# Storing three of four input groups by line, and reading them by unit

## The chip, the core and the metric

The kernel runs on one NeuronCore of a Trainium2 chip. The metric is device time in microseconds of that core; the kernel before takes 4201.34 us (median of three runs, 4199.3 to 4201.84).

## The reference

The input x is (32, 48, 64, 128), that is batch, channel, row h, column w, float32. Two layers follow each other. Each is `x = x + scnn(groupnorm(x))`, with its own weights:

```python
nxt = inp + conv1d(carry, w, b)      # 48 to 48 channels, 5 taps
```

The SCNN part runs this step along h from 0 to 63 (carry is a whole row, the taps run over w), then back from 63 to 0, then along w from 0 to 127 (carry is a column, the taps run over h), then back. Every step needs the one before it. The group norm has 16 groups of three channels and takes mean and variance over its channels and all of h and w, per image.

## The kernel before

**Tiling.** The 32 images are four groups of eight (`GB`). Channel and position modulo eight give 48 x 8 = 384 rows, three tiles `o` of 128 partitions; `PIECES` (L50) says which channels of which residue `e` lie where: ten pieces of 16, 32 or 48 partitions. A step (L876) is nine products of 128x128 on TensorE and three additions on VectorE (L898), one for each `o`.

**Phases.** `PHASES` (L103) are 12: eight "rows" phases (one image group each, 63 steps down and 63 up) and four "cols" phases (a pair of groups, 127 steps right and 127 left). This text counts them from 0. Their order is rows of layer 0 for groups 0 and 1, cols for that pair (phase 2), rows of group 2 (phase 3), rows of layer 1 for group 0 (phase 4), rows of layer 0 for group 3 (phase 5), cols for groups 2 and 3 (phase 6), rows of layer 1 for groups 1, 2, 3 (phases 7 to 9), and the two cols of layer 1. The tile names in the profile tell them apart: `step_02d` is layer 0, group 2, down.

**The input of layer 0.** An image group of x comes in as it lies in memory, 24 rows on each partition (`take_in`, tensor `in_x`). GpSimd copies two of these rows at a time into the order (quarter, residue, block, image) (`permute`, L650 to L659), and `put_out` (L661) stores each of the 24 permuted rows to a DRAM tensor `xin` of that group in one DMA of 128 partitions, 512 KB, issued on SyncE's queue SP. For group 0 this is done at the start, by GpSimd and ScalarE; for groups 1, 2 and 3 `plan_input` (L981) puts it beside the scans, through two tiles of two rows each. ScalarE takes the group's statistics from the same input tiles (`take_others`, L512).

**Reading it.** xin is laid out by (residue or row block, quarter), channel, and then a unit of 8 KB. It is read twice. A rows phase of layer 0 loads its 64 rows in four blocks of 16: `move_rows` (L679) issues 20 DMAs a block in runs of 128 bytes, ten for every eight rows. ScalarE then normalizes the block (`scale_rows`, L714, 24 ACTIVATE on L722, images outermost and `o` innermost), and the scan reads one row per step. A cols phase of layer 0 loads x again as a residual (`load_residual`, L810): for each quarter and each of six units (three `o`, two groups) it issues three or four DMAs, one for each piece, with 8 KB contiguous on each partition. GpSimd adds it (L824), `keep_result` (L826) stores the sum to `mid`, the input of layer 1, and statistics of the sum are taken. `mid` is laid out by quarter, line, (position, channel) and line content. Layer 1 reads it with `take_rows` (L702), which issues 40 DMAs for a block of 16 rows, one for each piece and quarter, in runs of 128 bytes, and with `by_unit` (L246), which covers a 1 MB unit of 128 partitions in one DMA, or two for the last `o`, in runs of 1 KB.

**What sets the order.** `at` (L968) enters work in an agenda under a time counted in steps; `catch_up` hands it out as the steps are traced, and `in_order` (L277) ties every instruction to the one before on its engine. Each queue therefore issues in program order. The agenda's time isn't waited for: a queue runs ahead until an instruction of it waits for data or for a buffer. Nearly all DMAs are on SP. The tile layer gives DMAs of SP and ScalarE eight completion semaphores in turn, and a DMA waits until the last one with its semaphore has landed, so that at most eight are in flight. `plan_rows` (L1001) places block loads and scalings of a rows phase: phase 1 loads at -34, -18, -3 and +12 steps of its start, a rows phase after a cols phase at -28, -12, 4 and 20, others at -54, -43, 0 and 11. It also places the stores of the finished up-scan (`upa`, ten DMAs for eight rows).

Of the kernel before, what the change touches and what calls it, by code (L numbers as in the profile page):

```python
# [29 lines left out]
F32 = mybir.dt.float32  # L30
# [3 lines left out]
C = 48  # L34
# [8 lines left out]
E8 = 8  # L43
FULL = 128
NG = E8 * C // FULL
NQ = 4
# [31 lines left out]
def weight_runs():  # L78
# [24 lines left out]
PHASES = (  # L103
    ("rows", 0, 0),
    ("rows", 0, 1),
    ("cols", 0, 0),
    ("rows", 0, 2),
    ("rows", 1, 0),
    ("rows", 0, 3),
    ("cols", 0, 1),  # L110
    ("rows", 1, 1),
# [8 lines left out]
def kernel(  # L120
# [8 lines left out]
    nc = tc.nc  # L129
    B, _, H, W = x.shape  # L130
    NK = W // E8
    NH = H // E8
# [4 lines left out]
    LINE = E8 * RUN  # L137
    UNIT = NH * LINE
    SLOT = 2 * NG * UNIT
    HALF = H // 2  # L140
    NGRP = B // GB
# [4 lines left out]
    PR = C * H // FULL  # L146
# [6 lines left out]
    dram = ctx.enter_context(tc.tile_pool(name="dram", bufs=1, space=bass.MemoryType.DRAM))  # L153
# [34 lines left out]
    def kept(name):  # L188
# [3 lines left out]
            for g in range(NGRP)  # L192
        ]

    source = [
        [
            dram.tile([E8 * NQ, C, UNIT], F32, tag=f"xin{g}", name=f"xin{g}")
            for g in range(NGRP)
        ],
        [  # L200
            dram.tile([NQ, NH, E8 * C, LINE], F32, tag=f"mid{g}", name=f"mid{g}")
            for g in range(NGRP)
        ],
    ]
    ups = [kept("upa"), kept("upb")]
    taps = [
# [28 lines left out]
    def x_by_col(t, e, j):  # L235


        return t[e * NQ + j]
# [7 lines left out]
    def by_unit(t, o, j):  # L246


        at = [(o * FULL, 0, FULL)]
        if o == NG - 1:  # L250
            at = [(6 * C, 0, 2 * C), (5 * C + C // 3, 2 * C, FULL)]
        t = t[j].rearrange("a m n -> m a n")
        return [(t[r : r + p1 - p0], p0, p1) for r, p0, p1 in at]

    def by_line(t):

        return t.rearrange("p (a n) -> p a n", a=NH)

    def x_put(t, r):


        t = t.rearrange("(i q) c (a n) -> i (c a) q n", i=E8, a=NH)[r % E8]
        return t.rearrange("(p r) q n -> r p q n", r=PR // E8)[r // E8]
# [6 lines left out]
    def dma(dst, src, queue=None):  # L270
        (queue or nc.sync).dma_start(dst, src)
# [34 lines left out]
    def pieces(o):  # L306
        return [(e, c0, c1, p0) for e, c0, c1, g, p0 in PIECES if g == o]
# [342 lines left out]
    def permute(nat, r0, perm, engines):  # L650
# [4 lines left out]
        for i in range(rows * NQ):  # L655
# [2 lines left out]
            copy = eng.copy if eng is nc.scalar else eng.tensor_copy  # L658
            copy(dst[:, r, q], src[:, r0 + r, q])  # L659

    def put_out(g, r, perm):  # L661


        n = perm.shape[-1] // (W * GB)
        for i in range(n):
            at = slice(i * W * GB, (i + 1) * W * GB)
            dma(
                x_put(source[0][g], r + i),
                perm[:, at].rearrange("p (q n) -> p q n", q=NQ),
            )  # L670


    def row_views(k):
# [2 lines left out]
    def row(k, h):  # L676
        return row_views(k)[h // HALF][:, :, h % HALF]
# [132 lines left out]
    def load_residual(k, j, i, nat):  # L810
        _, layer, pair = PHASES[k]
        o, half = UNITS[i]
        t = source[layer][2 * pair + half]
        if layer:
            for there, p0, p1 in by_unit(t, o, j):
                dma(by_line(nat)[p0:p1], there, nc.scalar)
        else:
            for e, c0, c1, p0 in pieces(o):
                dma(nat[p0 : p0 + c1 - c0], x_by_col(t, e, j)[c0:c1])
# [148 lines left out]
    def at(t, fn, *args):  # L968
        agenda.append((t, len(agenda), fn, args))
# [11 lines left out]
    def plan_input(g, times, work, lag, nats, perms):  # L981

        stats = InputStats(f"x{g}", 0)
        rows = nats[0].shape[-1] // W
        ahead, pieces_of = len(nats), rows * W // BN
        per = rows * W * GB // perms[0].shape[-1]
        for j, t in enumerate(times):
            nat = nats[j % ahead]
            if j == 0 and g > 1:
                at(t - 7, take_in, g, 0, nat)  # L990
            for i in range(per):
                perm, r = perms[i % len(perms)], i * rows // per
                at(t + i * work / per, permute, nat, r, perm, [nc.gpsimd])
                at(t + i * work / per + 4, put_out, g, rows * j + r, perm)
            at(t + lag, stats.take_others, pieces_of * j, nat)
            if j + ahead < len(times):
                free = t + 7
                at(free, take_in, g, rows * (j + ahead), nat)
        spread(t + work + lag + (0, 2, 32, 5)[g], scaling(f"x{g}", 0, g, stats, x_masks, (0, 0, 8, 0)[g]), 1)

    def plan_rows(k, t0, prev):  # L1001
        if k == 1:
            ahead, scaled = (-34, -18, -3, 12), (-12, -2, 17, 33)
        elif prev == "cols":
            ahead, scaled = (-28, -12, 4, 20), (-13, 3, 19, 35)
        else:
            ahead, scaled = (-54, -43, 0, 11), (-22, -8, 16, 30)
        if k:
            for i in range(4):
                if PHASES[k][1]:  # L1010
                    for o in range(NG):
                        t = t0 + ahead[i] - 2 + 3 * o
                        at(t, take_rows, k, i * LOAD, (i + 1) * LOAD, o)
                else:
                    at(t0 + ahead[i], move_rows, k, i * LOAD, (i + 1) * LOAD, False)
                at(t0 + scaled[i], scale_rows, k, i * LOAD, (i + 1) * LOAD)

        cuts = list(range(0, H + 1, E8))
        following = PHASES[k + 1][0] == "cols"
        seam = following and follows(k + 1)  # L1020
        if seam:
            cuts = cuts[2:]
            end = t0 + 2 * (H - 1)
            at(end - E8, move_rows, k, E8, 2 * E8, True, 0)
            for h in range(E8 - 1, -1, -1):
                at(end - h, send_row, k + 1, h, range(0, E8 // 2))
            at(end, send_rest, k + 1, range(E8 // 2, E8))
            for q in range(1, NQ):
                at(end + 0.1 if q == 1 else end + 1.6, move_rows, k, 0, 2 * E8, True, q)
        for h0, h1 in zip(cuts, cuts[1:]):  # L1030
            t = t0 + 2 * (H - 1) - h0
            if k == 0:
                t += 16 if h0 >= HALF else 68
            elif not following:
                t = t0 + 92 + 5 * (H - h1) / E8 + (34 if h1 <= HALF else 0)
            at(t, move_rows, k, h0, h1, True)
        at(
            t0 + H - 1,
            nc.gpsimd.tensor_copy,
            last.rearrange("p (o n) -> p o n", o=NG),  # L1040
            row(k, H - 1),
        )

    def follows(k):

        _, layer, pair = PHASES[k]
        return PHASES[k - 1] == ("rows", layer, 2 * pair + 1)

    def plan_cols(k, t0, prev):
# [44 lines left out]
        for u, (t, j, i) in enumerate(direct):  # L1094
            nat = tiles[u % n]
            o, half = UNITS[i]
            if u < n:
                at(left + 16, load_residual, k, j, i, nat)
            if layer == 0:
                if u >= n:  # L1100
                    at(direct[u - n][0] + 3, load_residual, k, j, i, nat)
                at(t, add_residual, k, j, i, nat)
                at(t + 4, keep_result, k, j, i)
                unit = quarter(k, j)[:, half, o]
                if half == 0:
                    for b in range(GB):
                        at(t + 5 + b, stats[0].take, j, o, unit, b)
                else:
                    at(t + 1, stats[1].take, j, o, unit)
            else:  # L1110

                at(t, add_residual, k, j, i, nat)
                at(t + 2.5, permute_unit, k, j, i, nat, (nc.gpsimd, nc.scalar, nc.scalar))
                if final or j not in HELD:
                    at(t + 4.5, store_result, k, j, i, nat)
                else:
                    at(t + 4.5, hold_result, j, i, nat)
                if final and j == 1:
                    at(t + 4.7, load_residual, k, 0, i, last_tiles(k)[i])

                if u >= 2 and u - 2 + n < len(direct):
                    at(t + 4.6, load_residual, k, *direct[u - 2 + n][1:], tiles[(u - 2) % n])
# [60 lines left out]
    def first_group():  # L1183
# [84 lines left out]
        def put_rows(*engines):  # L1268
            for eng in engines:
                r, perm = order[put[0]], tiles[put[0]]  # L1270
                put[0] += 1
                permute(parts[r // rows], r % rows, perm, (eng,))
                put_out(0, r, perm)
# [142 lines left out]
```

## Time and profile before

| | |
|---|---|
| profiled execution, device time | 4201.03 us |
| its span, first to last instruction | 4199.2 us |
| mean granted TensorE clock | 0.987 |
| GpSimd, ScalarE, VectorE busy | 19%, 31%, 51% |
| SP queue (q1): packets, data, share of 16 DMA engines | 2062096, 582.09 MB, 68.2% |
| ScalarE queue (q10) | 141424, 87.19 MB, 8.6% |
| stores to xin, 512 KB each | 96 |
| phase 1, 3, 4, 5, 7: TensorE's first step | 332.3, 1090.1, 1361.1, 1613.2, 2368.4 us |

Busy shares are of the span. In a timeline, a line is a run of like instructions: start, duration, engine, line of code, tensors, count; `SPq` is the SP queue, whose time is that of issuing, waits for semaphores included. A helper issues nearly all DMAs, so that they all carry one line of code (L271), and the tensors tell them apart. A window's row has the busy time of each engine, the granted clock, the busy share of the DMA engines and the data moved.

### The profile page before, as it was taken

The page shows a single profiled execution, that of the slowest core. Times are in us where ns is not written, and L with a number is a line of the kernel's source. Part 1 is how long each engine was busy: PE and PEld are TensorE (multiplying, and loading weights), DVE is VectorE, ACT ScalarE, POOL GpSimd, SP SyncE. Part 2 cuts the span into 40 slices and gives each one's busy share as a digit, 9 for nine tenths or more (in the row PEclk, how much of TensorE's full clock was granted, in tenths as well). Part 3 has the DMA queues.
Part 4 walks back from the last instruction along what each step waited for, and adds up shares of the span by engine and source line. Part 5 has one row for each costly group of instructions (what it writes and reads, how often), then busy time and mean ns, then how long its engine had stood idle before and what let it go on. Part 6 is the DMA issues. An engine that isn't in the chain of part 4 may idle for free. (4 is left out here: it accounts for less than half of the span.)

```text
span 4199.2 us, 90284 instructions
## 1 busy us (share of the span) xinstructions
PE 4083.1 (97%) x36724; PEld 4050.4 (96%) x36724; DVE 2133.5 (51%) x6501; ACT 1287.7 (31%) x2525; POOL 787.0 (19%) x737
## 2 busy tenths in 40 slices
PE   8999999999999999999999999999999999999994
PEld 6999999999989999999999989999999999999994
DVE  5454444456644454444457554444444444444444
ACT  6845000536874543000016762523000002200122
POOL 3520010434222000010023410000000006610253
PEclk9999999999999999999999999999999999999997
DMA  9987669669969999258419968948379019999799
GB/s 293 235 178 115 110 125 209 210 162 250 206 186 165 168 166 157 36 104 195 99 44 264 187 142 140 139 65 141 64 130 212 14 51 232 287 253 160 152 237 197
DMA packets 2206497, 680.57 MB, mean 162 GB/s; under 512 B 2008465, under 2 KB 2157185, under 8 KB 2179969
## 3 DMA queue, kind: packets, MB, share of 16 engines
q1 hardware_dynamic: 2062096, 582.09, 68.2%
q10 hardware_dynamic: 141424, 87.19, 8.6%
q8 instruction: 289, 4.73, 0.5%
q0 software_dynamic: 2560, 5.51, 0.5%
q14 instruction: 128, 1.04, 0.1%
HBM read 397.77 MB, written 295.14 MB: 165 GB/s over the span
## 5 line engine op out<-in xcount | busy, mean ns | idle before, releaser
L722 ACT ACTIVATE arena<-arena,offset,scale 128x256 f32<-128x256 f32 (+2 forms) x840 | 582.5, 789 | 377.2 <-DMA arena<-mid 230.7
L824 POOL TENSOR_TENSOR arena<-arena 128x2048 f32<-128x2048 f32 x80 | 362.8, 4548 | 1456.3 <-PE step_10l L889 463.1
L659 POOL COPY arena<-arena 128x256 f32<-128x256 f32 x332 | 196.7, 657 | 460.3 <-DMA arena<-in_x 407.5
L597 ACT ACTIVATE early<-arena 128x256 f32<-128x256 f32 x192 | 129.5, 675 | 442.0 <-POOL arena L824 436.1
L889 PE MATMUL step_00r<-arena,early 128*128 128x128 f32 x2286 | 252.1, 274 | 6.1 <-DMA arena<-arena 5.8
L889 PEld LDWEIGHTS step_00r<-arena,early 128*128 128x128 f32 x2286 | 251.4, 185 | 6.8 <-issue 5.6
L889 PE MATMUL step_01r<-arena,early 128*128 128x128 f32 x2286 | 251.9, 274 | 6.2 <-DMA arena<-arena 5.2
L889 PEld LDWEIGHTS step_01r<-arena,early 128*128 128x128 f32 x2286 | 251.1, 185 | 7.0 <-issue 5.5
L889 PE MATMUL step_00l<-arena,wleft 128*128 128x128 f32 x2286 | 249.2, 272 | 0.0
L889 PE MATMUL step_11r<-arena,early 128*128 128x128 f32 x2286 | 249.2, 272 | 0.0
L889 PEld LDWEIGHTS step_11r<-arena,early 128*128 128x128 f32 x2286 | 248.7, 184 | 0.4 <-DVE arena L898 0.3
L889 PEld LDWEIGHTS step_00l<-arena,wleft 128*128 128x128 f32 x2286 | 248.7, 184 | 0.0
L889 PE MATMUL step_11l<-arena,wleft 128*128 128x128 f32 x2286 | 248.5, 272 | 0.0
L889 PE MATMUL step_10l<-arena,wleft 128*128 128x128 f32 x2286 | 248.5, 272 | 0.0
L889 PE MATMUL step_01l<-arena,wleft 128*128 128x128 f32 x2286 | 248.4, 272 | 0.0
L889 PE MATMUL step_10r<-arena,early 128*128 128x128 f32 x2286 | 248.4, 272 | 0.0
L889 PEld LDWEIGHTS step_11l<-arena,wleft 128*128 128x128 f32 x2286 | 248.4, 184 | 0.0
L889 PEld LDWEIGHTS step_10l<-arena,wleft 128*128 128x128 f32 x2286 | 248.4, 184 | 0.0
L889 PEld LDWEIGHTS step_01l<-arena,wleft 128*128 128x128 f32 x2286 | 248.4, 184 | 0.0
L889 PEld LDWEIGHTS step_10r<-arena,early 128*128 128x128 f32 x2286 | 248.4, 184 | 0.0
L282 ACT COPY early<-arena 128x1 f32<-128x1 f32 x2 | 0.4, 192 | 697.3 <-DVE arena L898 697.3
L846 ACT COPY arena<-arena 128x256 f32<-128x256 f32 x172 | 99.8, 657 | 362.5 <-POOL arena L824 277.2
(200 smaller groups left out, 7089.5 us busy)
## 6 DMA issues: line engine op xcount, KB each, us to landing
xin<-arena SPq DMA_DIRECT2D x91, 512.0 KB, 4.2
arena<-in_x SPq DMA_DIRECT2D x18, 2048.0 KB, 11.3
arena<-xin SPq DMA_DIRECT2D x96, 384.0 KB, 10.2
arena<-mid SPq DMA_DIRECT2D x384, 96.0 KB, 3.1
upb<-arena SPq DMA_DIRECT2D x192, 192.0 KB, 3.9
arena<-upb SPq DMA_DIRECT2D x96, 384.0 KB, 13.2
arena<-xin SPq DMA_DIRECT2D x180, 192.0 KB, 4.4
mid<-arena SPq DMA_DIRECT2D x32, 1024.0 KB, 10.6
```

Source lines behind the costliest of these rows:

```text
L282: fn(*args)
L597: nc.scalar.activation(junk[:, 0:n], view[:, b], AF.Identity, accum_out=self.sum[:, i, j : j + 1])
L659: copy(dst[:, r, q], src[:, r0 + r, q])
L722: nc.scalar.activation(args[0], args[0], AF.Identity, bias=args[2], scale=args[1])
L824: eng.tensor_tensor(unit, unit, nat, ALU.add)
L846: copy(by_w(perm)[:, a], src[:, a])
L889: nc.tensor.matmul(part(whole(ps[o])[0:m], -s), weights[:, i, at : at + m], part(src(i), s), start=seen[o] == 1, stop=seen[o] == left[o],)
```

## The change

The tensors xin of groups 1, 2 and 3 take the layout that mid has. Group 0 keeps its own.

```diff
+    def by_lines(name):
+
+        return dram.tile([NQ, NH, E8 * C, LINE], F32, tag=name, name=name)
+
     source = [
         [
-            dram.tile([E8 * NQ, C, UNIT], F32, tag=f"xin{g}", name=f"xin{g}")
+            by_lines(f"xin{g}")
+            if g
+            else dram.tile([E8 * NQ, C, UNIT], F32, tag=f"xin{g}", name=f"xin{g}")
             for g in range(NGRP)
         ],
...
+    def put_lines(t, r, perm):
+
+
+        i, runs = r % E8, PR // E8
+        t = t.rearrange("q a (i c) n -> i a c q n", i=E8)[i]
+        for first in range(E8):
+            c, a = divmod(runs * first + r // E8, E8)
+            dma(t[a, c : C : runs], perm[first : FULL : E8])
+
     def put_out(g, r, perm):
...
-            dma(
-                x_put(source[0][g], r + i),
-                perm[:, at].rearrange("p (q n) -> p q n", q=NQ),
-            )
+            whole = perm[:, at].rearrange("p (q n) -> p q n", q=NQ)
+            if g:
+                put_lines(source[0][g], r + i, whole)
+            else:
+                dma(x_put(source[0][g], r + i), whole)
...
         t = source[layer][2 * pair + half]
-        if layer:
+        if layer or pair or half:
             for there, p0, p1 in by_unit(t, o, j):
-                dma(by_line(nat)[p0:p1], there, nc.scalar)
+                dma(by_line(nat)[p0:p1], there, nc.scalar if layer else None)
...
-                if PHASES[k][1]:
+                if PHASES[k][1:] != (0, 0):
                     for o in range(NG):
                         t = t0 + ahead[i] - 2 + 3 * o
                         at(t, take_rows, k, i * LOAD, (i + 1) * LOAD, o)
```

So for groups 1 to 3 a permuted row goes out in eight DMAs of 16 partitions and 64 KB, still in runs of 1 KB; a residual unit comes in by one or two DMAs in runs of 1 KB, still on SP; and the row blocks of phases 1, 3 and 5 are loaded by `take_rows`, 40 DMAs a block in three portions, one for each `o`, which stand at -2, +1 and +4 steps of where the whole block stood.

More of the change, by code (lines that the diff above doesn't have):

```diff
@@ L193, in kept @@
         ]
+    def by_lines(name):
+        return dram.tile([NQ, NH, E8 * C, LINE], F32, tag=name, name=name)
     source = [
         [
-            dram.tile([E8 * NQ, C, UNIT], F32, tag=f"xin{g}", name=f"xin{g}")
+            by_lines(f"xin{g}")
+            if g
+            else dram.tile([E8 * NQ, C, UNIT], F32, tag=f"xin{g}", name=f"xin{g}")
             for g in range(NGRP)
         ],
[L200 to L203, printed above, removed]
+        [by_lines(f"mid{g}") for g in range(NGRP)],
     ]
```

## The prediction, before the changed kernel was run

> **What bounds the kernel now.** First the page's busy times and slices:
>
> ```profile
> PE 4083.1 (97%) x36724; PEld 4050.4 (96%) x36724; DVE 2133.5 (51%) x6501; ACT 1287.7 (31%) x2525; POOL 787.0 (19%) x737
> ...
> PE   8999999999999999999999999999999999999994
> ...
> DMA  9987669669969999258419968948379019999799
> ```
>
> TensorE sets the time, and nothing in the change touches its work. The change can only remove or make stalls of the scans. Those show in the phases' lengths, from the tiles of the down-scans (first start, last start of 63 steps):
>
> ```profile
> L889 PEld LDWEIGHTS step_01d<-arena,early x1134: 163/192/193, 332.1 to 456.5; 128*128 128x128 f32 x126, 128*96 128x96 f32 x63
> L889 PEld LDWEIGHTS step_02d<-arena,early x1134: 162/192/338, 1090.0 to 1230.5; 128*128 128x128 f32 x126, 128*96 128x96 f32 x63
> L889 PEld LDWEIGHTS step_11d<-arena,early x1134: 163/192/338, 2368.3 to 2519.8; 128*128 128x128 f32 x126, 128*96 128x96 f32 x63
> L889 PEld LDWEIGHTS step_12d<-arena,early x1134: 163/192/193, 2649.7 to 2775.1; 128*128 128x128 f32 x126, 128*96 128x96 f32 x63
> ```
>
> A clean scan takes some 125 us (1.98 a step). Phase 3 takes 140.5 and phase 7 151.5: 15.5 and 26.5 us are stalls. Both follow a cols phase whose residual loads share SP with the row blocks. In phase 7 ScalarE's scaling of rows 16 to 31 shows what is late:
>
> ```profile
> 2375.85 0.86 ACT L722 ACTIVATE arena<-arena,offset,scale 128x256 f32<-128x256 f32 x1
> 2378.69 0.85 ACT L722 ACTIVATE arena<-arena,offset,scale 128x256 f32<-128x256 f32 x1 [1.98 <-DMA arena<-mid]
> 2393.22 16.39 ACT L722 ACTIVATE arena<-arena,offset,scale 128x256 f32<-128x256 f32 x22 [13.68 <-DMA arena<-mid]
> ```
>
> The third instruction needs the last o, so a block is ready 16.5 us after its last portion lands, here at 2409.6; row 16 was due at 2368.4 + 15 x 1.98 = 2398. Next, SP before phase 1, where group 1 is stored:
>
> ```profile
> 181.22 7.42 SPq L271 DMA_DIRECT2D xin<-arena  x4
> ...
> 202.02 33.41 SPq L271 DMA_DIRECT2D xin<-arena  x14
> 235.52 10.85 SPq L271 DMA_DIRECT2D upa<-arena  x10
> 246.47 1.35 SPq L271 DMA_DIRECT2D xin<-arena  x2
> 251.74 20.28 SPq L271 DMA_DIRECT2D arena<-xin  x20
> 272.11 21.12 SPq L271 DMA_DIRECT2D upa<-arena  x20
> ```
>
> From 181 to 450 SP hardly rests. Phase 1 doesn't stall: its blocks are scaled at 298.5 and 334.7, due at 332.3 and 362.
>
> **What the skill says.** "DMA: Bandwidth & Descriptors", section "Rules for kernel authors": small transfers should be joined; under 64 KB one pays mostly overhead. The trace agrees: DMAs of 6 KB from SP stand 0.46 us apart at the closest, 1 MB ones 0.47. "SBUF — State Buffer", section "Door 1: The DMA port swizzle", says that bandwidth depends on how many of 16 ports the partitions reach, and partitions 0 to 63 reach half of them. Piece loads of 16 to 48 partitions (first row) against units of 128 (second) agree:
>
> ```profile
> 866.00:880.00 14.00, 14.00 (x131) 14.00 (x131) 7.02 (x23) 0.00 (x0) 0.00 (x0) 1.00 1.02 179
> 3412.00:3422.00 10.00, 10.00 (x95) 10.00 (x93) 4.80 (x15) 0.00 (x0) 0.00 (x0) 1.00 1.04 331
> ```
>
> Both have the DMA engines full; the last number is GB/s. "TensorE: Matmul & The Clock Gate", Part 1: an idle TensorE falls to half clock and needs some 3.4 us of work to recover. Phase 3's first two steps after its stall take 3.95 and 3.0 us instead of 1.97, so I add 3 us to each new stall.
>
> **The stores.** Of 72 stores each becomes eight: 504 more DMAs on SP. Bytes and runs stay, so the DMA engines don't feel it; SP does. A DMA of 64 descriptors isn't in the trace. Bounds: 0.41 us (shortest issue of a 512 KB store, 0.36, and the gap of 0.05) and 0.57 (a row DMA of mid). I take the floor of small DMAs, 0.47: 3.76 us a row. GpSimd needs less:
>
> ```profile
> 178.74 18.98 POOL L659 COPY arena<-arena 128x256 f32<-128x256 f32 x32
> ```
>
> That is eight rows, 2.37 each. So SP, not GpSimd, paces the stores. Group by group:
>
> *Group 1.* 24 x 3.76 = 90.2 us from 181.2; two loads of in_x in between, 1 us, and 4 us each until the semaphores behind a 2 MB load come free (9.4 to land, less the 3.3 in which seven stores go out; bounds 0 and 6); ten upa stores, 10.9; landing 2.2. The first row load starts at 293.5 instead of 251.7. A block by take_rows is 24.5 us:
>
> ```profile
> 1234.47 13.06 SPq L271 DMA_DIRECT2D early<-taps  x25
> ...
> 1285.78 3.46 SPq L271 DMA_DIRECT2D xin<-arena  x4
> ...
> 1364.09 49.04 SPq L271 DMA_DIRECT2D arena<-mid  x80
> ```
>
> 80 DMAs, two blocks; 40 DMAs of the old form take some 43, so reading costs 3 us more a block. But by the agenda the portions stand at steps 90, 93, 96, and upa stores at 94, 102 and 110: ten now fall ahead of the last portion. Block 0: 293.5 + 17.2 (28 DMAs) + 10.9 + 7.4 = 329.0, landed 332, scaled 348.5: 16 us late. Block 1 has the stores of 102 ahead and those of 110 inside: 329.0 + 10.9 + 17.2 + 10.9 + 7.4 = 375.4, scaled 394.9, due at 348.5 + 29.7 = 378.2: 17 more. Blocks 2 and 3 make it (419 against 426). Phase 1 loses 33 + 2 x 3 = 39 (bounds 20 and 55).
>
> *Group 2.* SP waits there for in_x and ScalarE; each four rows take 15 us instead of 7.4 and delay the next load by some 4.5, the last row by 27, to 886. The residuals that follow are added from 902 on, and the first lands within 6 us. Nothing; without this cover it would be under 10.
>
> *Group 3.* Rows 0 to 3 fall in an idle stretch. Rows 4 to 7 and 8 to 11 go out as in the fence, 3.4 us for four; now 15 each: +23 for SP's row blocks of phase 4. Rows 32 to 47 are scaled at 1407.8, due at 1361.1 + 31 x 1.99 = 1423: 15 us of slack. Late by 8, + 3 = 11 (bounds 0 and 18). The last 12 rows put SP some 55 us back before phase 5, whose rows 32 to 47 had 54 us of slack plus the 8 of phase 4: nothing, at most 7.
>
> **The residuals.** At 179 GB/s a unit of 1 MB takes 5.8 us of all DMA engines, at 331 3.2. Phase 2 has 10 such units after the first four, phase 6 has 20: 26 and 52 us less, and four DMAs for ten in SP's way. What is late in the stalls: in phase 3 rows 32 to 47, landed at 1151.6 and due (16.5 before the row) at 1135; in phase 7 rows 16 to 31, 2393 against 2381.5, then rows 32 to 47, 2438 against 2413. The relief exceeds each lack. What is late next is ScalarE's order of scaling and statistics (18 and 13.7 us in turn): it makes row 32 of phase 7 at 2426 against 2430. The portions, however, put a residual load ahead of the last o. I take 12 of phase 3's 15.5 (bounds 0 and 15.5) and 23 of phase 7's 26.5 (bounds 8 and 26.5).
>
> **The sum.** +39 + 11 - 12 - 23 = +15 on the profiled execution's 4201.0 (span 4199.2, 1.8 around it), 0.3 below the median of the runs: 4216.
>
> **Rivals.** *The reads win.* If an eighth of a row costs SP 0.41 us and in_x holds nothing up, phase 1's block 0 is in time, block 1 13 us late, 16 with the clock; phase 4 loses 7; the full 41 or so come back: 4184. It decides at about 0.41 us a store: 15 us over 192 DMAs for phase 1 and 64 for phase 4. For it: eight small DMAs leave the engines free. Against: no DMA of the trace goes out closer than 0.46. *The reads give nothing,* because the stalls of phases 3 and 7 come from order (a portion behind a residual that waits for GpSimd): +50, 4251. For it: SP waits 253.6 us for the residual additions. Against: the waits of ScalarE there end with DMAs, with the engines full. *Even.* Both sides within 8 us of each other: 4203.
>
> **How the numbers follow.** About 0.2%, 8.4 us, is what a measurement of this kernel can tell from no change. Forecast of a net loss 0.42; reads give nothing 0.12; even 0.18; reads win 0.28. So slower 0.54, same 0.18, faster 0.28. Range: 4183 takes in the reads winning, 4254 nearly all of the case with nothing back; the loss alone would be 4210 to 4240.
>
> **What would show it.** Right: stores to xin 0.47 us apart; phase 1 some 164 us down instead of 124.4, with TensorE idle ahead of rows 1 and 16; phase 3 near 128, phase 7 near 129, phase 4 near 136; residual units at over 300 GB/s. Wrong: phase 1 without a stall, or phases 3 and 7 as before.

## The result, and the profile after

The changed kernel takes 4342.4 us (median of four runs, 4332.8 to 4349.9) where the kernel before takes 4201.6 beside it: 1.033 times, 95% interval 1.0305 to 1.0355. The forecast was 4216, with 4254 as its upper end. The profiled execution is 4349.94 us with a span of 4348.2 and a mean granted clock of 0.972, to be set against 4201.03, 4199.2 and 0.987: 148.9 us more. It is the slowest of the four; by the medians the difference is 140.8 us. Lines of the changed kernel's code stand 3 to 13 below those of before (L271 is now L274, L659 is L662, L722 is L735, L824 is L837, L889 is L902, L898 is L911).

The page after, busy times and slices:

```profile
PE 4102.7 (94%) x36724; PEld 4066.9 (94%) x36724; DVE 2137.8 (49%) x6501; ACT 1286.9 (30%) x2525; POOL 787.0 (18%) x737
...
PE   8994999998988988999999999999999999999994
...
DMA  9748677749985866946914896957649317999799
```

The work of the engines is the same; TensorE now has gaps in slices 4, 10, 12, 13, 15 and 16, and the DMA engines are busy for five to nine tenths of these, so TensorE does not wait there for full DMA engines. The scans' tiles of the changed kernel say which (first start, last start):

```profile
L902 PEld LDWEIGHTS step_01d<-arena,early x1134: 163/192/338, 379.6 to 521.4; 128*128 128x128 f32 x126, 128*96 128x96 f32 x63
L902 PEld LDWEIGHTS step_02u<-arena,early x1134: 163/192/337, 1329.4 to 1473.2; 128*128 128x128 f32 x126, 128*96 128x96 f32 x63
L902 PEld LDWEIGHTS step_10d<-arena,early x1134: 163/192/337, 1473.3 to 1622.5; 128*128 128x128 f32 x126, 128*96 128x96 f32 x63
L902 PEld LDWEIGHTS step_10u<-arena,early x1134: 163/192/338, 1622.6 to 1768.2; 128*128 128x128 f32 x126, 128*96 128x96 f32 x63
L902 PEld LDWEIGHTS step_11d<-arena,early x1134: 163/192/338, 2529.3 to 2668.6; 128*128 128x128 f32 x126, 128*96 128x96 f32 x63
```

Phase 1 starts 47.5 us later and takes 141.8; phase 3 up, phase 4 down and phase 4 up take 143.8, 149.2 and 145.6 where some 125 to 130 were enough; phase 7 down takes 139.3, better than 151.5 but not the 129 of the forecast. SP ahead of phase 1, in the changed kernel:

```profile
181.17 21.64 SPq L274 DMA_DIRECT2D xin<-arena  x32
...
203.71 24.67 SPq L274 DMA_DIRECT2D xin<-arena  x32
...
229.81 79.50 SPq L274 DMA_DIRECT2D xin<-arena  x112
309.41 9.89 SPq L274 DMA_DIRECT2D upa<-arena  x10
319.40 10.98 SPq L274 DMA_DIRECT2D xin<-arena  x16
330.62 15.79 SPq L274 DMA_DIRECT2D arena<-xin  x28
346.51 9.13 SPq L274 DMA_DIRECT2D upa<-arena  x10
355.68 7.13 SPq L274 DMA_DIRECT2D arena<-xin  x12
```

The order is the one that the prediction worked out (28 loads, ten upa stores, 12 loads), but the first row load goes out at 330.6 and not at 293.5. Over all 576 stores the median from one issue to the next is 0.64 us, not 0.47.

### The profile page after: what moved, and what is told of

The parts are those of the page before. It is cut to its first block, busy times and chain, and to the rows that moved or that the text cites. A ratio compares the mean times of both kernels' runs of the same rounds, so it can differ in the third digit from the quotient of the medians.

```text
span 4348.2 us, 91103 instructions
## 1 busy us (share of the span) xinstructions
PE 4102.7 (94%) x36724; PEld 4066.9 (94%) x36724; DVE 2137.8 (49%) x6501; ACT 1286.9 (30%) x2525; POOL 787.0 (18%) x737
## 5 line engine op out<-in xcount | busy, mean ns | idle before, releaser
L735 ACT ACTIVATE arena<-arena,offset,scale 128x256 f32<-128x256 f32 (+2 forms) x840 | 581.9, 788 | 532.3 <-DMA arena<-mid 239.8
L837 POOL TENSOR_TENSOR arena<-arena 128x2048 f32<-128x2048 f32 x80 | 362.5, 4546 | 1422.4 <-PE step_10l L902 473.3
L662 POOL COPY arena<-arena 128x256 f32<-128x256 f32 x332 | 196.8, 647 | 657.7 <-DMA arena<-in_x 485.8
L902 PE MATMUL step_00l<-arena,wleft 128*128 128x128 f32 x2286 | 251.2, 273 | 21.0 <-DVE arena L911 21.0
L902 PEld LDWEIGHTS step_00l<-arena,wleft 128*128 128x128 f32 x2286 | 250.4, 185 | 21.2 <-DVE arena L911 21.2
L902 PE MATMUL step_00r<-arena,early 128*128 128x128 f32 x2286 | 253.8, 275 | 9.3 <-DMA arena<-arena 5.7
L902 PEld LDWEIGHTS step_00r<-arena,early 128*128 128x128 f32 x2286 | 253.1, 186 | 10.0 <-issue 5.0
L902 PE MATMUL step_01r<-arena,early 128*128 128x128 f32 x2286 | 253.6, 275 | 9.3 <-DMA arena<-arena 5.5
L902 PEld LDWEIGHTS step_01r<-arena,early 128*128 128x128 f32 x2286 | 252.9, 186 | 10.0 <-issue 5.5
L902 PE MATMUL step_11r<-arena,early 128*128 128x128 f32 x2286 | 249.3, 272 | 0.3 <-DVE arena L911 0.3
L902 PEld LDWEIGHTS step_11r<-arena,early 128*128 128x128 f32 x2286 | 248.6, 184 | 0.8 <-DVE arena L911 0.8
L902 PE MATMUL step_10l<-arena,wleft 128*128 128x128 f32 x2286 | 248.5, 272 | 0.0
L902 PE MATMUL step_01l<-arena,wleft 128*128 128x128 f32 x2286 | 248.5, 272 | 0.0
L902 PE MATMUL step_11l<-arena,wleft 128*128 128x128 f32 x2286 | 248.5, 272 | 0.0
L902 PE MATMUL step_10r<-arena,early 128*128 128x128 f32 x2286 | 248.5, 272 | 0.0
L902 PEld LDWEIGHTS step_10l<-arena,wleft 128*128 128x128 f32 x2286 | 248.4, 184 | 0.0
L902 PEld LDWEIGHTS step_01l<-arena,wleft 128*128 128x128 f32 x2286 | 248.4, 184 | 0.0
L902 PEld LDWEIGHTS step_11l<-arena,wleft 128*128 128x128 f32 x2286 | 248.4, 184 | 0.0
L902 PEld LDWEIGHTS step_10r<-arena,early 128*128 128x128 f32 x2286 | 248.4, 184 | 0.0
```

What stands on the lines that cost most here:

```text
L735: nc.scalar.activation(args[0], args[0], AF.Identity, bias=args[2], scale=args[1])
L837: eng.tensor_tensor(unit, unit, nat, ALU.add)
L902: nc.tensor.matmul(part(whole(ps[o])[0:m], -s), weights[:, i, at : at + m], part(src(i), s), start=seen[o] == 1, stop=seen[o] == left[o],)
```

## The experiments

Theory A: the price of the stores on SP makes the whole loss. Theory B: the loads by portion and unit make a good part of it. All ratios are against the kernel before on the same chip in the same session (4208.9 to 4210.4 us there). Where a kernel is said to use other positions, its values land in or come from other places of the same tensor; the count, size and runs of the loads are those of the kernel it is made from. Lengths of scans below are taken to the end of the last matmul, some 0.2 us more than in the tile lines.

**One store a row in the changed kernel.**

```diff
     def put_lines(t, r, perm):
-        i, runs = r % E8, PR // E8
-        ...
+        dma(t.rearrange("q a m n -> q (a m) n").rearrange("q (p r) n -> r p q n", r=PR)[r], perm)
```

> The changed kernel with each row of groups 1 to 3 stored by one DMA of 128 partitions instead of eight, to the same tensor but to other places in it: the values read back belong to other positions, so the output isn't the reference's; number, shape and order of all loads are those of the changed kernel. Theory A (the price of the stores on SP makes the whole loss; what is late elsewhere is late because SP is): no stall in phase 1, none in phases 2, 4 and the statistics, 4165 to 4195 us. Theory B (the loads by portion and the unit loads make a good part of the loss): 4230 us or more, with phase 4 still over 140 us down.

Measured: 4212.9 us, 1.0007 (0.9998 to 1.0015). The loss is gone, so it is the split of the stores (A). But no gain is left: phase 7 down is 10 us shorter than before and phase 3 down 10 us longer. (Phase 6 right is 6 us longer too, but that comes and goes in kernels of both kinds; see *Open* below.) The new loads are worth nothing net, which A hadn't expected.

**The split alone, in the kernel before.** Old places, old loads, eight stores of every eighth partition for groups 1 to 3:

```diff
-            dma(
-                x_put(source[0][g], r + i),
-                perm[:, at].rearrange("p (q n) -> p q n", q=NQ),
-            )
+            there, here = x_put(source[0][g], r + i), perm[:, at].rearrange("p (q n) -> p q n", q=NQ)
+            for part in (slice(f, FULL, E8) for f in range(E8)) if g else (slice(0, FULL),):
+                dma(there[part], here[part])
```

> The kernel before with only the stores changed: each row of groups 1 to 3 goes out in eight DMAs of every eighth partition, to the places of before. Theory A: about as slow as the changed kernel plus what its reads give back, 4340 to 4390 us, stores 0.64 us apart. Theory B: under 4260 us.

Measured: 4344.2 us, 1.0322 (1.0305 to 1.0338); stores 0.64 us apart. Nothing else of the change is needed for the loss, with the old loads. Whether it is all a matter of the price of a store, as A has it, is the question of the next runs.

**Eight stores of 16 adjacent partitions**, otherwise the same:

```diff
-            for part in (slice(f, FULL, E8) for f in range(E8)) if g else (slice(0, FULL),):
+            for part in (slice(16 * f, 16 * f + 16) for f in range(E8)) if g else (slice(0, FULL),):
```

> As the run before, but each of the eight DMAs takes 16 partitions that lie side by side, to the places of before. If the step of eight partitions is what makes a store cost 0.64 us rather than 0.47: stores 0.47 us apart, 4250 to 4300 us. If it is the small store of 64 runs as such, or the three-fold pattern in DRAM: 0.64 us, the same time as the run with every eighth partition.

Measured: 4261.1 us, 1.012 (1.0098 to 1.0141); stores 0.47 apart. So many, so large, and 83 us cheaper; 27 of these 83 are in phase 4 down and have a cause of their own (*Group 3* below). Its timeline on SP, to be compared with the changed kernel's (both x112 stretches hold the same waits of the prefetch):

```profile
184.90 16.35 SPq L271 DMA_DIRECT2D xin<-arena  x32
...
223.18 61.41 SPq L271 DMA_DIRECT2D xin<-arena  x112
```

**Which step costs it.** A slice of every eighth partition also steps over places in DRAM. Two kernels take the steps apart; the values land in other positions:

```diff
-                dma(there[part], here[part])
+                dma(there[f:FULL:E8], here[16 * f : 16 * f + 16])
+                dma(there[16 * f : 16 * f + 16], here[f:FULL:E8])
```

> The kernel before with eight stores for each permuted row of groups 1 to 3, each from 16 adjacent partitions to every eighth place in DRAM, so that values land in other positions. If the step on the side of the partitions is what takes the stores from 0.47 to 0.64 us apart: 0.47 here, and 1.012 as with adjacent partitions and adjacent places. If it is the step in DRAM: 0.64 and 1.032.

> The counterpart: each of the eight stores from every eighth partition to 16 adjacent places in DRAM, so that values land in other positions. Step on the side of the partitions: 0.64 us apart, 1.032. Step in DRAM: 0.47, 1.012. If both steps are needed: 0.47 in both of these runs.

Measured: step in DRAM 4257.9 us, 1.0114 (1.0084 to 1.0143), stores 0.47 apart; step in SBUF 4351.7, 1.0336 (1.0306 to 1.0366), 0.64 apart. SP in the first and in the second:

```profile
223.01 61.46 SPq L271 DMA_DIRECT2D xin<-arena  x112
```

```profile
232.04 78.92 SPq L271 DMA_DIRECT2D xin<-arena  x112
```

So the step over partitions alone sets the 0.64 us. (The 94 us between the two kernels hold the added wait of *Group 3* too.)

**Group by group.** The split of every eighth partition for one group at a time (`if g == 1`, and so on, for `if g`):

> The kernel before, with eight stores of every eighth partition for each permuted row of group 1 alone; groups 2 and 3 keep one store a row. Theory A (each group's stores hurt where they stand, and the losses add up): +52 us, all of it at the start of phase 1 and in its down-scan, as in the run with all three groups so split; 1.012 times before. Rival C (the losses are one lateness of SP that is carried on): less than half of the 138 us shows here in phase 1, and stalls in phases 2 to 4 are there as well though groups 2 and 3 are as before; over 1.018.

> The kernel before, with eight stores of every eighth partition for each permuted row of group 2 alone. Theory A: one stall of some 24 us in the left scan of phase 2 and nothing else, +26 us, 1.006. Rival C: the stall needs SP's lateness from group 1, and this run is within 5 us of before. My prediction's step for this group was nothing.

> The kernel before, with eight stores of every eighth partition for each permuted row of group 3 alone. Theory A: stalls of some 11, 22 and 16 us in the up-scan of phase 3, the down-scan of phase 4 and its up-scan, and a few us of low clock: +60 us, 1.014. Rival C: less than +40, since a phase that starts on time leaves SP the slack that the run with all three groups split hadn't. My prediction had 11 us for this group.

Measured: 4258.0 us, 1.0119 (1.0104 to 1.0135); 4241.5, 1.0075 (1.0058 to 1.0093); 4267.6, 1.0145 (1.012 to 1.0171). The losses add up (1.0339 by the three, 1.0322 all together), and each stands where A said. Group 1: phase 1 starts 40 us later, its down-scan takes 13 more. Group 2: one stall of 22 us in the left scan of phase 2, and 5 us more each in phase 2 right and phase 3 down, which A had not said. Group 3: stalls of 13 us in phase 3 up, 23 in phase 4 down, 14 and 2 in phase 4 up. Rival C (one lateness carried on) falls.

**The new loads beside stores at the predicted price.** The changed kernel, with each row put out in eight transfers of 16 adjacent partitions:

```diff
+        there = t.rearrange("q a m n -> q (a m) n").rearrange("q (p r) n -> r p q n", r=PR)[r]
+        for f in range(0, FULL, 16):
+            dma(there[f : f + 16], perm[f : f + 16])
```

> The changed kernel, with each permuted row of groups 1 to 3 put out by eight transfers of 16 adjacent partitions to other places of the same tensor: stores that go out 0.47 us apart instead of 0.64, and the new loads. The values read back are from other positions. If my sum was right but for the price of a store (which was 0.47): 4216, 1.003 to 1.004, with 35 us given back in phases 3 and 7. If the sum was wrong in the reads and in the steps that I took for nothing too: the +52 us that the same stores cost beside the old loads, and no more than 5 us back, 1.011 to 1.013.

Measured: 4273.7 us, 1.0159 (1.0143 to 1.0174). That is neither: with the price of the forecast granted, the kernel is 63 us slower than before by the medians (74 by the two traces) where the sum has 15, and the new loads are a little worse than the old ones beside the same stores (1.0159 against 1.012).

**Where the gain of the loads went.** First the blocks of phases 1, 3 and 5 in one go, with one store a row:

```diff
-                        t = t0 + ahead[i] - 2 + 3 * o
+                        t = t0 + ahead[i] - (2 - 3 * o) * (PHASES[k][1] > 0)
```

> The changed kernel with one store a row (as in the run with one store, so again with values from other positions), and the blocks of 16 rows of phases 1, 3 and 5 loaded in one go where they stood before, not in three portions at -2, +1 and +4 steps. Theory P (the order of the portions ate the gain of the residual loads: something else gets ahead of the last o): phase 3 down falls from 150.7 to about 132, as with two copies, and the left-over 6 us of phase 6 go; some 4188, 0.995 times before. Rival Q (40 transfers a block in place of 20 take SP and the DMA engines longer, whatever their order): phase 3 stays at 145 or more, 4205 to 4213, 0.999 to 1.001.

Measured: 4206.8 us, 0.999 (0.9983 to 0.9996); phase 3 down 143.0. The order of the portions cost 7.7 us of 150.7 (7 us by the ratios), not the 19 of theory P. The time is the one that Q gave. Then the loads of both sorts at their best: each row stored twice, once as before for the row blocks, once to a tensor of its own for the residual, one transfer each:

```diff
+    again = [
+        dram.tile([NQ, E8 * C, UNIT], F32, tag=f"xres{g}", name=f"xres{g}") if g >= 1 else None
+        for g in range(NGRP)
+    ]
...
             dma(x_put(source[0][g], r + i), whole)
+            if again[g] is not None:
+                dma(q_put(again[g], r + i), whole)
...
+        elif again[2 * pair + half] is not None:
+            for there, p0, p1 in q_unit(again[2 * pair + half], o, j):
+                dma(nat[p0:p1], there)
```

`q_put` and `q_unit` are the places of a row and the one or two ranges of a unit in a tensor of (quarter, position and channel, line content), so that a residual has 8 KB runs on up to 128 partitions.

> The kernel before, with a second copy of the permuted rows of groups 1 to 3 in a tensor laid out by quarter, position and channel, one DMA of 128 partitions a row; residual loads of these groups read it as units of 128 partitions with 8 KB each, one or two DMAs. Stores of before stay, and row blocks load as before. If wider residual loads relieve the DMA engines: phase 7 some 10 to 25 us shorter than 151.8, phase 3 up to 12 shorter, 4165 to 4190 us, though 72 more stores of about 0.4 us stand on SP. If they don't (the stalls come from order): 4200 to 4215 us.

Measured: 4190.8 us, 0.9957 (0.9943 to 0.997). **Faster than both kernels.** Its tiles:

```profile
L908 PEld LDWEIGHTS step_02d<-arena,early x1134: 163/192/338, 1093.4 to 1225.5; 128*128 128x128 f32 x126, 128*96 128x96 f32 x63
L908 PEld LDWEIGHTS step_11d<-arena,early x1134: 163/192/338, 2372.6 to 2506.2; 128*128 128x128 f32 x126, 128*96 128x96 f32 x63
```

132.1 and 133.6 us, where before had 140.5 and 151.5. Phase 4 up pays 9 us for it. Last, two copies again, the second in the changed kernel's shape, read as a residual from other positions in runs of 1 KB:

```diff
-        dram.tile([NQ, E8 * C, UNIT], F32, tag=f"xres{g}", name=f"xres{g}") if g >= 1 else None
+        dram.tile([NQ, NH, E8 * C, LINE], F32, tag=f"xres{g}", name=f"xres{g}") if g >= 1 else None
...
-            for there, p0, p1 in q_unit(again[2 * pair + half], o, j):
-                dma(nat[p0:p1], there)
+            for there, p0, p1 in by_unit(again[2 * pair + half], o, j):
+                dma(by_line(nat)[p0:p1], there)
```

> The kernel with two copies of groups 1 to 3 (row blocks from the old form in 20 transfers a block), the second copy in the changed kernel's shape and read as a residual as the changed kernel reads it, in runs of 1 KB, from other positions, so that the sums hold values from other places. Theory R (the row blocks of 40 transfers are what keeps phase 3 at 143 us where two copies had 132.3): phase 3 down at 132 to 134 and 0.996. Rival S (the runs of 1 KB against 8 KB are): phase 3 at 140 to 143, phase 7 down at 142 against 133.9, 1.000.

Measured: 4199.9 us, 0.9975 (0.996 to 0.999). The five kernels together (us, down-scans):

| kernel, a row in one transfer | row blocks of phase 3 | residual | phase 3 | phase 7 |
|---|---|---|---|---|
| before | 20 transfers | 8 KB runs, 16 to 48 partitions | 140.8 | 151.8 |
| two copies | 20 | 8 KB, up to 128 partitions | 132.3 | 133.9 |
| two copies, by line | 20 | 1 KB, up to 128 | 135.2 | 140.0 |
| block at once | 40 at once | 1 KB, up to 128 | 143.0 | 142.7 |
| one store | 40 in portions | 1 KB, up to 128 | 150.7 | 141.7 |

Each length is from one trace. In the traces with the old loads and group 2 stored as before, phase 3 down varies from 137.8 to 143.3, and with the old loads phase 7 down from 150.1 to 156.9, so a step of some 3 us is not shown. Wider residual loads do help, by 8.5 and 17.9 us. Then 1 KB runs take back 6 in phase 7 (the 3 in phase 3 is not shown), 40 transfers a block 8 in phase 3, and the portions 8 more there. Theory R fits phase 3, S phase 7.

**The second copy on ScalarE's queue** (`nc.scalar` as the third argument of its store), a try at the 9 us of phase 4 up:

> The kernel with two copies of groups 1 to 3 (old rows, wide residual loads), the second copy's store issued on ScalarE's queue and not on SP. If its 9 us of stall in the up-scan of phase 4 come from SP, which is behind with group 3's last input load: they go, 4182, 0.993. Rival: ScalarE now waits for the permute and is late with scaling; phases 1 and 4 lose over 10 us, 1.000 or more.

Measured: 4221.9 us, 1.0032 (1.0021 to 1.0043). The rival's losses are there: phase 1 starts 10 us later than with both copies on SP, and phase 4 up takes 153.5 in place of 136.0. In phase 4 up the input's statistics on ScalarE now wait 19.2 us for a store of the second copy; in phase 1 ScalarE's part was not followed.

## Why the prediction was wrong

By the places of its sum (us against the trace of before, the start of a phase counted with its first scan):

| | on record | stores 0.47 us apart, new loads | changed kernel |
|---|---|---|---|
| phase 1, start and down | +39 | +41 | +65 |
| phase 2 | 0 | +5 | +28 |
| phase 3 down | -12 | +9 | +6 |
| phase 3 up | 0 | +9 | +14 |
| phase 4 down | +11 | 0 | +24 |
| phase 4 up | 0 | +20 | +19 |
| phase 7 down | -23 | -11 | -12 |
| sum, with some 5 elsewhere in the last column | +15 | +73 | +149 |

The last column less the second is what the step over partitions did, some 75 us: 24 of them are an added wait in phase 4 down, so the price of a store made some 50. The second less the first is what was wrong besides, some 58 (48 by the medians).

*TensorE sets the time, and only stalls of the scans change.* Right: the phases hold the whole difference.

*"I take the floor of small DMAs, 0.47."* This step failed: 0.64, outside its bounds of 0.41 and 0.57. Each of the rows that gave the floor and the upper bound is a transfer of adjacent partitions. None in the trace of before steps over partitions, and that is what the change adds; at adjacent partitions 0.47 is met to the digit. As a floor it was misread all the same: it is a common interval, and single DMAs in the trace of before follow after 0.35 us.

*Group 1.* The path was right, and the price is most of what the term missed. With 0.47 it is 41 for 39, in part by luck: ScalarE ends the scaling of blocks 0 and 1 at 356.7 and 404.0, some 8 and 9 us later than the 348.5 and 394.9 on record, and the first stall is larger than forecast, the second a little smaller. The first two lines are of that run, the last two of the changed kernel, which ends these blocks at 381.0 and 426.8, another 24 and 23 us later. Its 192 stores cost 0.17 x 192 = 33 us more, of which 29 reach the first row load (330.6 against 301.9).

```profile
340.49 16.25 ACT L733 ACTIVATE arena<-arena,offset,scale 128x256 f32<-128x256 f32 x22 [17.48 <-DMA arena<-xin]
...
386.26 17.77 ACT L733 ACTIVATE arena<-arena,offset,scale 128x256 f32<-128x256 f32 x24 [18.09 <-DMA arena<-xin]
```

```profile
364.72 16.25 ACT L735 ACTIVATE arena<-arena,offset,scale 128x256 f32<-128x256 f32 x22 [14.93 <-DMA arena<-xin]
...
408.95 17.80 ACT L735 ACTIVATE arena<-arena,offset,scale 128x256 f32<-128x256 f32 x24 [17.19 <-DMA arena<-xin]
```

*Group 2, "Nothing; without this cover it would be under 10".* The cover is there at 0.47 (the left scan keeps its 250.9 us) and is used up at 0.64. SP's timeline of the changed kernel:

```profile
941.49 22.68 SPq L274 DMA_DIRECT2D xin<-arena  x32
964.27 0.54 SPq L274 DMA_DIRECT2D arena<-in_x  x1
974.79 20.55 SPq L274 DMA_DIRECT2D xin<-arena  x32
995.44 13.40 SPq L274 DMA_DIRECT2D arena<-xin  x12
```

A round of four rows, its load included, takes 33 us where before had 21 to 22; on record it grew by 4.5. So the stores end 86 us after the left scan's start, the residuals come behind them, and additions were due after 63 (902 in the trace of before). At 0.47 (old loads) the round is 27.5 us and they end after 61. Nor is the price of the lost cover "under 10". The waits from 970 to 1015 us:

```profile
POOL arena L837 <- DMA arena<-xin: 22.5, 2, 21.3
DVE bn_r L576 <- POOL arena L837: 21.7, 1, 21.7
...
PE step_00l L902 <- DVE arena L911: 21.0, 1, 21.0
```

GpSimd waits for the residual, VectorE's statistics instruction of the sum waits for GpSimd, and the step's additions are queued behind it. So a late residual stalled the scan, though no step reads it.

*Group 3.* Phase 4 down was +11 on record: 0 at 0.47, +24 at 0.64. The 24 come neither from the price nor from late row blocks, which is how the forecast reasoned. They stand before row 48. In the changed kernel ScalarE scales rows 48 to 63 only when 16 stores to xin have landed that SP issues after these rows' loads:

```profile
1540.54 19.89 SPq L274 DMA_DIRECT2D upa<-arena  x20
1560.54 10.85 SPq L274 DMA_DIRECT2D xin<-arena  x16
```

```profile
1572.90 17.71 ACT L735 ACTIVATE arena<-arena,offset,scale 128x256 f32<-128x256 f32 x24 [38.46 <-DMA xin<-arena]
```

With adjacent partitions and the same loads, it scales them when their loads are there, ahead of these stores:

```profile
1491.27 16.45 ACT L733 ACTIVATE arena<-arena,offset,scale 128x256 f32<-128x256 f32 x22 [6.75 <-DMA arena<-mid]
```

```profile
1509.22 8.74 SPq L274 DMA_DIRECT2D xin<-arena  x16
```

The last of the row loads of the changed kernel landed at 1542.2 and ScalarE was idle, so without this wait the rows would have been ready at some 1560 (an estimate: 17.7 us of scaling), 8 us before the stall begins. The run with adjacent partitions has the same work without the wait, so the data don't need it; it stands in the program of each kernel that stores group 3 from every eighth partition (stalls of 21 to 23 us before row 48). Why it gets there isn't shown. So the step over partitions costs twice: in the price of a store, and in a wait.

Missed were also the up-scans of phases 3 and 4, 28 us even at 0.47. In the changed kernel GpSimd stands in the permute until the next rows of in_x have landed. SP issues that load only behind the 32 stores of rows 4 to 7, and it lands at 1376.4. The group norm's small steps stand behind the permute:

```profile
1346.43 20.86 SPq L274 DMA_DIRECT2D xin<-arena  x32
1367.39 1.26 SPq L274 DMA_DIRECT2D arena<-in_x  x1
```

```profile
1376.83 4.67 POOL L662 COPY arena<-arena 128x256 f32<-128x256 f32 x8 [33.55 <-DMA arena<-mid]
1381.45 0.36 POOL L622 TENSOR_TENSOR neg_r<-neg_r,mean_r_r 128x96 f32<-128x96 f32 x1
```

The profile puts this wait down to a load of mid, the last DMA by its reckoning. The waits from 1360 to 1390 go on from there:

```profile
DVE var_r_r L632 <- POOL neg_r L628: 12.7, 1, 12.7
...
PE step_02u L902 <- DVE arena L911: 11.4, 1, 11.4
```

In phase 4 up it is the input's statistics on ScalarE, late because the last load of in_x waits on SP behind stores (1630 to 1670 us):

```profile
ACT early L531 <- DMA arena<-in_x: 25.4, 1, 25.4
...
PE step_10u L902 <- DVE arena L911: 15.5, 2, 12.7
DVE mean_x_x L548 <- ACT early L531: 13.0, 1, 13.0
```

The prediction asked only when rows are ready for the scans. It didn't follow the statistics, which have later due times but share VectorE with the step. That is the second failed step: "nothing" where a late input meets an engine whose work is queued in order, in phases 2 (21 us), 3 (11) and 4 (13).

*The residuals.* The mechanism is right, the sizes aren't. "The relief exceeds each lack" took 2.6 us a unit (5.8 less 3.2). In the six units of phase 6 that follow the first four, from first issue to last landing, before takes 45.5 us, the block-at-once kernel 37.6: 1.3 a unit, half. `mid` is stored in the same time, and the first of these units go out 4.5 us apart in both kernels, which is the time of one addition on GpSimd (4.56), so the loads alone don't set the pace; how much each takes isn't shown. The port rule of the Trainium skill ("SBUF — State Buffer", section "Door 1: The DMA port swizzle") agrees in its direction; with 8 KB runs on 128 partitions it is 34.2. In phase 3 the step "I take 12" failed altogether: the portions, named there as a doubt, and the 40 transfers a block, counted there at 3 us, eat more than the relief.

*Rivals.* "The reads give nothing" came nearest, by 91 us still; its reason, the order, is shown for phase 3 only. "The reads win" decides at 0.41 us a store, and no kernel here with eight stores a row came near that. Its counter, that no DMA of the trace goes out closer than 0.46, is a misreading: of the 2260 DMAs on SP that follow another directly, 104 do so in under 0.455 us.

*Open.* Phases 2 and 6 right take 253 us in some kernels and 258 in others, with a wait of 4 to 5 us for a DMA within arena at the start; no part of the change decides it. That phase 4 up is 9 us longer with two copies was read from its wait for statistics and not undone. No kernel stored group 3 from every eighth partition without the wait on ScalarE, so the two costs of the step are parted by the traces and not by a run.

## What to carry to other kernels

Before pricing a split transfer, find a row of the same shape, the partitions' step included; if there is none, the nearest row is no bound. Then read in the new program's trace what each engine waits for: a new access pattern can bring a wait that the data don't need. Where a queue goes from resting to full, list what else passes through it (inputs of statistics, loads that GpSimd waits for), and follow each to the engine that works in order and feeds the bottleneck. A layout for one reader can be had without touching the other: a second copy in one transfer a row cost less than eight transfers of one copy.

## What the runs showed of the hardware

- A DMA of 16 partitions with 4 KB each, issued by SP, goes out 0.47 us after the last with adjacent partitions and 0.64 with every eighth partition; a step of eight in DRAM costs nothing (0.47). The time is spent in issuing: 0.42 us of each interval with adjacent partitions and 0.59 with every eighth (medians). Both land after some 2.0 us.
- A DMA of 128 partitions and 512 KB was followed by the next after 0.40 us (two copies, 1199.6 us), so the bytes aren't what sets this interval.
- At up to 128 partitions, the same six residual units take 36.1 to 37.6 us with runs of 1 KB (five kernels) and 34.2 to 34.4 with runs of 8 KB (two).
